# The order of three accumulated slots inside a convolution step

## The chip, the cores and the metric

The kernel runs on one core of a Trainium2 chip. The metric is the device time of one execution in microseconds (us); the median of several executions is compared, and one execution is profiled.

## What is computed

The reference is a chain of four layers on x of shape (4, 32, 32, 16). Each layer first normalises x over groups of two channels and all pixels (`_gn`) and adds its result to x. Layers 0, 1 and 3 have the same core, and nearly all the time is theirs:

```python
first   = jnp.einsum('ijyx,byxc->bijc', Msq, inputs)
shifted = lax.conv_general_dilated(x_nchw, kern, STRIDES, PADDING)   # a 3x3 kernel for each of 32*32*16 outputs
diff    = jax.nn.relu(inputs[:, None, None, :, :, :] - shifted)
second  = L * jnp.einsum('ijyx,bijyxc->bijc', Wsq, diff)
return first - second
```

For each of 1024 output positions (i, j) and 16 channels f there is an own 3x3 kernel over 16 input channels. It is run over the whole 32x32 image, the result is subtracted from the normalised input, cut at zero, weighted with 1024 weights and summed to one number. Layer 2, the interval layer, is a small dynamic program over pairs (i, j), and takes little time of its own.

## The kernel before, in words

The four images are handled as two groups of two (NG, GB). The three convolution layers for two groups make six phases, run one after the other by `conv_layer` (line 436). What the next phase needs (normalisation, the unrolled image, the interval layer) and the `first` term are issued in small pieces between the steps of the running phase: `behind` is a generator, and after each step it is asked for its next piece when a count of steps (`wait`) has run down. The order on every engine is therefore written by hand.

The image is unrolled into `im`: 128 partitions, 64 for each half of the image (16 rows of pixels, 512 pixels). In the 64 partitions of a half stand four taps times 16 input channels. Slot 0 of `im` holds taps 0 to 3, slot 1 taps 4 to 7, and slot 2 the ninth tap alone, four copies of its 16 channels. The kernels' coefficients come in `raw` in the same layout, for a unit of eight output channels and 128 output positions at a time (`load_raw`, line 74, three units ahead, four buffers).

Slots 0 and 1 are multiplied in float32. The profile counts two matmul passes for each such matmul. The ninth tap uses its four copies for another way to float32 accuracy: the tensors `W9` (from `raw`) and `im9` (from `im`) are of type float32r and hold the rounded values in some copies and the remainders in others, so one pass adds up the partial products. They are made by `halve` on ScalarE (line 111) and `halve_rest` on VectorE (line 114). For the weights that is `prep` (line 134, called at the second of a unit's eight channels for the next unit) and `prep_rest` (line 149, called at the fifth); `prep` also lets GpSimd subtract `pick` from slot 1 (line 140), which brings in the input itself. For the image it stands at the end of `before_conv` (lines 232 and 234). At the start of the kernel both pairs are made before step 0: `im9`, then `prep(0)` and `prep_rest(0)` (lines 517 and 518). The loads of slot 2 of `im` are issued first in `before_conv`, then those of taps 0 to 7.

A step is one output channel f and one image b for 128 output positions: six matmuls of 64 x 128 by 512 pixels, three slots for each of two halves (line 463), into a pair of PSUM banks `ps` (three pairs, line 58). The two halves use different halves of TensorE's rows and different banks. Then VectorE takes the pair of banks in one instruction (`scalar_tensor_tensor`, line 473: the smaller of the value and zero, times the 1024 weights of `WT`, summed into a column of `acc`). There are 6 phases x 8 tiles x 16 channels x 2 images = 1536 steps. Between steps TensorE also gets the matmuls of `first_term` (`pf`, line 248, and `pfs`, line 256), and those of the interval layer (`ps_r`, `ps_l`, `ps_y`).

In a step, the first matmul starts the sum in its bank (`start`), and so it is the one that waits until VectorE has read the pair of banks three steps before; the last one (`stop`) tells VectorE to begin. The instructions of a step on TensorE are issued in the order of the loops, and that is the order that the change touches.

Of the kernel before, what the change touches and what calls it, by code (L numbers as in the profile page):

```python
# [37 lines left out]
def net_kernel(ctx: ExitStack, tc: tile.TileContext, x, convs, iv_w, iv_b, out):  # L38
# [19 lines left out]
    def bank_pair(name):  # L58
        return psum.tile([P, 2, 512], F32, tag="ps", name=name)
# [14 lines left out]
    def load_raw(u):  # L74
        if u < n_chunks * NU:
            n = u // NU
            raws[u] = wpool.tile([P, 3, FU, P], F32, tag="raw", bufs=4, name=f"raw_{u}")
            nc.sync.dma_start(raws[u], convs[phases[n // NT][1]][2][n % NT, u % NU])

    def load_chunk(n):  # L80
        if n < n_chunks:
            t = n % NT
            chunks[n] = wpool.tile([P, NP], F32, tag="WT", name=f"WT_{n}")
            nc.sync.dma_start(chunks[n], convs[phases[n // NT][1]][1][t * P : (t + 1) * P, :])
# [49 lines left out]
    def prep(u):  # L134

        if u >= n_chunks * NU:
            return
        raw = raws.pop(u)
        f0 = u % NU * FU
        nc.gpsimd.tensor_tensor(  # L140
            raw[:, 1], raw[:, 1],
            pick[:, f0 : f0 + FU].unsqueeze(2).to_broadcast([P, FU, P]),
            ALU.subtract,
        )
        W9 = wpool.tile([P, FU, P], F32R, tag="W9", name=f"W9_{u}")
        halve(W9, raw[:, 2], low_w)
        units[u] = (raw, W9)

    def prep_rest(u):
        if u in units:  # L150
            raw, W9 = units[u]
            halve_rest(W9, raw[:, 2], low_w)
# [52 lines left out]
    def before_conv(g, layer, on_pe=False):  # L205
        xn = work.tile([P, NT, GC], F32, tag="xn", bufs=2, name=f"xn_{g}_{layer}")
        xns[g] = xn
        yield from group_norm(g, f"c{g}{layer}", xn, on_pe)

        nc.vector.transpose(
            xt[g][:, :, 1 : 1 + H], xn
        )
        inner = xs[g][:, HP : HP + H * HP].rearrange("p (t r n) -> p r t n", r=ROWS, n=HP)
        for r in range(ROWS):
            (nc.scalar if r % 2 else nc.sync).dma_start(inner[:, r], xt[g][GC * r : GC * (r + 1)])
        yield 2
        xsv = xs[g].rearrange("(b c) n -> c b n", b=GB)
        at = 0  # L220
        for slot, row, tap in [(2, row, 8) for row in range(4)] + [
            (tap // 4, tap % 4, tap) for tap in range(8)
        ]:
            for h in range(2):
                off = (HI * h + tap // 3) * HP + tap % 3
                r0 = 64 * h + C * row
                (nc.scalar, nc.sync)[at % 2].dma_start(  # L227
                    im[g][r0 : r0 + C, slot, :, :RUN], xsv[:, :, off : off + RUN]
                )
                at += 1  # L230
        yield 9
        halve(im9[g], im[g][:, 2], low_x)
        yield 2
        halve_rest(im9[g], im[g][:, 2], low_x)
# [201 lines left out]
    def conv_layer(phase, behind):  # L436

        g, layer = phases[phase]
        wait = 0
        imv = im[g].rearrange("p s b (y x) -> p s b y x", x=HP)  # L440
        im9v = im9[g].rearrange("p b (y x) -> p b y x", x=HP)
        acc = work.tile([P, NT, GC], F32, tag="acc", bufs=2, name=f"acc_{phase}")
        for t in range(NT):
            n = phase * NT + t
            for f in range(C):
                u = n * NU + f // FU
                if f % FU == 1:
                    prep(u + 1)
                    load_raw(u + 3)
                if f % FU == 4:  # L450
                    prep_rest(u + 1)
                if f == 2:
                    load_chunk(n + 1)
                W, W9 = units[u]
                for b in range(GB):


                    ps = bank_pair(f"pc_{n}_{f}_{b}")
                    for slot in range(3):
                        for h in range(2):  # L460
                            r = slice(64 * h, 64 * h + 64)
                            w, v = (W9[r], im9v[r, b]) if slot == 2 else (W[r, slot], imv[r, slot, b])
                            nc.tensor.matmul(  # L463
                                ps[:, h, :],
                                lhsT=w[:, f % FU, :],
                                rhs=v[:, :, :H],
                                start=slot == 0,
                                stop=slot == 2,
                            )

                    col = b * C + f
                    junk = work.tile([P, NP], F32, tag="junk", name=f"junk_{n}_{col}")
                    nc.vector.scalar_tensor_tensor(  # L473
                        junk,
                        ps.rearrange("p h n -> p (h n)"),
                        0.0,
                        chunks[n],
                        op0=ALU.min,
                        op1=ALU.mult,
                        accum_out=acc[:, t, col : col + 1],  # L480
                    )
                    wait -= 1
                    if wait <= 0:
                        wait = next(behind, 1 << 20)
            nc.vector.tensor_tensor(X[g][:, t], X[g][:, t], acc[:, t], ALU.add)  # L485
        for _ in behind:
            pass
# [21 lines left out]
    start = before_conv(*phases[0], on_pe=True)  # L509
# [9 lines left out]
    for phase in range(len(phases)):  # L519
        conv_layer(phase, behind(phase))  # L520
# [64 lines left out]
```

## Time and profile before

| | us |
|---|---|
| median of 4 executions | 3105.47 (3105.25 to 3106.09) |
| the profiled execution | 3105.36 |
| its span, first to last instruction | 3103.6 |
| TensorE busy with matmuls (PE) | 3071.3 (99%) |
| TensorE loading weights (PEld) | 1534.2 (49%) |
| VectorE busy (DVE) | 2116.0 (68%) |
| GpSimd (POOL) | 294.7 (9%) |
| ScalarE (ACT) | 145.7 (5%) |

The span is split into engines: PE are matmul passes, PEld the loads of their weights, which run beside them. Two passes of the two halves run side by side, so the sum of the durations of all passes is larger than the busy time. A row of the costliest groups reads: line, engine, operation, output <- inputs, shape, count | busy time, mean duration in ns | idle time of the engine just before such instructions, and what ended most of it. A row of the order of time reads: start and duration in us, engine, line, operation, tensors, count, and in brackets the idle time before it with what ended it. Consecutive instructions of one kind are merged into one row. In the rows `pc<-im,raw` is a float32 pass of slot 0 or 1, and `pc<-im,W` the ninth tap's pass.

### The profile page before, as it was taken

The numbers are of one execution on the slowest core, as the hardware profiler recorded it, in microseconds if no ns is written. First come the engines' busy times: TensorE is split into PE (matmuls) and PEld (weight loads), VectorE is DVE, ScalarE is ACT, GpSimd is POOL, SyncE is SP. The second block draws the span as 40 slices with busy tenths as digits, with TensorE's granted clock in tenths as the row PEclk, the third lists the DMA queues.
The fourth block names the chain that finished last, engine by engine and source line by source line (L and its number), as shares of the span: only waits on it lengthen the run. The fifth ranks groups of instructions, "written<-read, shape, count | busy, mean of one in ns | idle before, by whom it ended". The sixth has DMA issues, their size and how long they took to land.

```text
span 3103.6 us, 37902 instructions
## 1 busy us (share of the span) xinstructions
PE 3071.3 (99%) x15760; PEld 1534.2 (49%) x15760; DVE 2116.0 (68%) x3361; ACT 145.7 (5%) x151; POOL 294.7 (9%) x182
## 2 busy tenths in 40 slices
PE   6999999999999999999999999999999999999999
PEld 4644444444444444444445444444544444444444
DVE  4666666766666666666678876668876666666666
ACT  0000000000000000000000000000000000000000
POOL 1100000100000000000012310001330000000000
PEclk9999999999999999999999999999999999999999
DMA  4331111321111141211111114121113211121100
GB/s 143 125 120 57 48 69 48 125 75 61 55 53 70 48 146 48 75 48 68 48 51 72 48 69 125 48 75 48 68 48 106 95 48 70 48 75 48 68 28 2
DMA packets 37069, 215.19 MB, mean 69 GB/s; under 512 B 11809, under 2 KB 12321, under 8 KB 23073
## 3 DMA queue, kind: packets, MB, share of 16 engines
q1 hardware_dynamic: 29472, 207.02, 18.5%
q10 hardware_dynamic: 7296, 5.74, 0.8%
q8 instruction: 123, 2.02, 0.3%
q14 instruction: 50, 0.40, 0.0%
q0 software_dynamic: 128, 0.02, 0.0%
HBM read 211.64 MB, written 1.12 MB: 69 GB/s over the span
## 4 chain that ended last, share of the span: by engine, by line
PE 99%; DMA 1%; DVE 0%; issue 0%; ACTq 0%; ACT 0%; DVEq 0%
PE pc L463 97%; PE pf L248 1%; PE pfs L256 0%; DMA im<-xs 0%; DMA X<-in_x 0%; DVE junk L473 0%; PE ps_r L376 0%; DMA xs<-xt 0%; PE ps_l L365 0%; PE ps_l L363 0%; DVE xc_c L188 0%; DVE pp L323 0%; ACTq L227 0%; PE ps_y L427 0%; PE ps_vc L178 0%
## 5 line engine op out<-in xcount | busy, mean ns | idle before, releaser
L463 PE MATMUL pc<-im,raw 64*128 64x512 f32 x12288 | 2913.2, 589 | 16.3 <-DMA im<-xs 14.5
L473 DVE SCALAR_TENSOR_TENSOR junk<-pc,WT 128x1024 f32<-128x1024 f32 x1536 | 1880.1, 1224 | 958.7 <-PE pc L463 953.0
L463 PEld LDWEIGHTS pc<-im,raw 64*128 64x128 f32 x12288 | 1209.4, 186 | 1165.7 <-issue 775.0
L463 PE MATMUL pc<-im,W 64*128 64x512 f32 x3072 | 1257.9, 804 | 0.0
L463 PEld LDWEIGHTS pc<-im,W 64*128 64x128 f32 x3072 | 304.8, 186 | 359.6 <-issue 352.2
L140 POOL TENSOR_TENSOR raw<-raw,pick 128x1024 f32<-128x1024 f32 x96 | 182.7, 1905 | 1988.4 <-DMA raw<-in_g 1863.9
L111 ACT ACTIVATE W<-raw,low_w 128x1024 fp32r<-128x1024 f32 x96 | 110.4, 1150 | 2270.6 <-PE pc L463 2234.5
L114 DVE SCALAR_TENSOR_TENSOR W<-raw,low_w,W 128x1024 fp32r<-128x1024 f32 x96 | 136.0, 1416 | 0.0
L473 DVE DVE_READ_ACCUMULATOR junk<-pc,WT 128x1 f32 x1536 | 127.8, 83 | 0.0
L396 POOL TENSOR_TENSOR dp_a<-ft_a,rt_r 128x1089 f32<-128x1089 f32 x16 | 39.1, 2447 | 76.3 <-DVE s_a L403 49.5
L396 POOL TENSOR_TENSOR dp_b<-ft_b,rt_r 128x1089 f32<-128x1089 f32 x16 | 37.1, 2326 | 94.6 <-ACT ft_b L389 47.8
L248 PE MATMUL pf<-MT,xn 128*32 128x512 f32 x192 | 23.1, 598 | 0.0
L403 DVE TENSOR_REDUCE s_b<-dp_b 128x33 f32<-128x1089 f32 x16 | 20.5, 1282 | 0.0
L403 DVE TENSOR_REDUCE s_a<-dp_a 128x33 f32<-128x1089 f32 x16 | 20.5, 1282 | 0.0
L175 POOL PARTITION_ALL_REDUCE sum_mc<-part_mc x5 | 2.2, 447 | 191.5 <-DVE part_mc L167 191.5
L252 ACT COPY fs<-pf 128x512 f32<-128x512 f32 x12 | 7.0, 586 | 240.7 <-PE pf L248 240.7
L114 DVE SCALAR_TENSOR_TENSOR im<-im,low_x,im 128x1088 fp32r<-128x1088 f32 x6 | 8.1, 1348 | 14.0 <-DMA im<-xs 14.0
L485 DVE TENSOR_TENSOR X<-X,acc 128x32 f32<-128x32 f32 x48 | 11.9, 247 | 1.5
L256 PEld LDWEIGHTS pfs<-stack,fs 128*128 128x128 f32 x96 | 11.2, 191 | 3.4 <-issue 3.4
L338 DVE TENSOR_TENSOR pp<-pp 64x1024 f32<-64x1024 f32 x10 | 12.1, 1212 | 0.0
L343 DVE TENSOR_TENSOR pp<-pp 64x1024 f32<-64x1024 f32 x10 | 12.1, 1212 | 0.0
L248 PEld LDWEIGHTS pf<-MT,xn 128*32 128x32 f32 x192 | 5.0, 109 | 14.0 <-issue 14.0
(77 smaller groups left out, 132.9 us busy)
## 6 DMA issues: line engine op xcount, KB each, us to landing
raw<-in_g SPq DMA_DIRECT2D x96, 1536.0 KB, 6.7
WT<-in_w SPq DMA_DIRECT2D x48, 512.0 KB, 6.5
MT<-in_mt SPq DMA_DIRECT2D x12, 2048.0 KB, 8.2
im<-xs SPq DMA_DIRECT2D x72, 67.8 KB, 3.0
im<-xs ACTq DMA_DIRECT2D x72, 67.8 KB, 3.1
xs<-xt SPq DMA_DIRECT2D x12, 34.0 KB, 2.9
xs<-xt ACTq DMA_DIRECT2D x12, 34.0 KB, 3.1
X<-in_x ACTq DMA_DIRECT2D x2, 128.0 KB, 5.1
```

The costliest lines, as they stand in the source:

```text
L111: nc.scalar.activation(dst, src, AF.Copy, scale=mask[:, 1:2])
L114: nc.vector.scalar_tensor_tensor(dst, src, mask[:, 0:1], dst.bitcast(F32), op0=ALU.mult, op1=ALU.add)
L140: nc.gpsimd.tensor_tensor(raw[:, 1], raw[:, 1], pick[:, f0 : f0 + FU].unsqueeze(2).to_broadcast([P, FU, P]), ALU.subtract,)
L248: nc.tensor.matmul(ps[32 * j : 32 * j + 32, :], lhsT=xn[:, pt, :], rhs=mt[:, pt, :], start=pt < 4, stop=pt >= 4, tile_position=(0, 32 * j),)
L256: nc.tensor.matmul(ps[:, GC * t : GC * (t + 1)], lhsT=fs[:, t // 4, t % 4 * P : (t % 4 + 1) * P], rhs=stack, start=True, stop=True,)
L338: nc.vector.tensor_tensor(pp[k][:, :H, M:], a[:, :H, M:], a[:, s : H + s, M:], ALU.max)
L343: nc.vector.tensor_tensor(pp[k][:, :H, M:], a[:, :H, M:], a[:, :H, M - s : M - s + H], ALU.max)
L396: nc.gpsimd.tensor_tensor(t, ft[:, i, :].unsqueeze(1).to_broadcast([P, T1, T1]), rt, ALU.add,)
L403: nc.vector.tensor_reduce(s[:, i - 1, :], last, axis=AX.X, op=ALU.max)
L463: nc.tensor.matmul(ps[:, h, :], lhsT=w[:, f % FU, :], rhs=v[:, :, :H], start=slot == 0, stop=slot == 2,)
L473: nc.vector.scalar_tensor_tensor(junk, ps.rearrange("p h n -> p (h n)"), 0.0, chunks[n], op0=ALU.min, op1=ALU.mult, accum_out=acc[:, t, co ...
L485: nc.vector.tensor_tensor(X[g][:, t], X[g][:, t], acc[:, t], ALU.add)
```

## The change

The loop over the slots runs in the order 2, 0, 1 in place of 0, 1, 2. The ninth tap's matmuls now start the sum in their bank, and those of slot 1 end it. Nothing else is changed; the number of instructions of each kind stays as it is.

```diff
-                    for slot in range(3):
+                    for k, slot in enumerate((2, 0, 1)):
                         for h in range(2):
                             r = slice(64 * h, 64 * h + 64)
                             w, v = (W9[r], im9v[r, b]) if slot == 2 else (W[r, slot], imv[r, slot, b])
@@
                                 ps[:, h, :],
                                 lhsT=w[:, f % FU, :],
                                 rhs=v[:, :, :H],
-                                start=slot == 0,
-                                stop=slot == 2,
+                                start=k == 0,
+                                stop=k == 2,
                             )
```

## The prediction

> **What bounds the kernel now.** I read the page from the top, then the chain that ended last, the costliest groups, and last the order of time in three stretches. The chain and the groups:
>
> ```profile
> PE 99%; DMA 1%; DVE 0%; issue 0%; ACTq 0%; ACT 0%; DVEq 0%
> ...
> L463 PE MATMUL pc<-im,raw 64*128 64x512 f32 x12288 | 2913.2, 589 | 16.3 <-DMA im<-xs 14.5
> L473 DVE SCALAR_TENSOR_TENSOR junk<-pc,WT 128x1024 f32<-128x1024 f32 x1536 | 1880.1, 1224 | 958.7 <-PE pc L463 953.0
> ...
> L463 PE MATMUL pc<-im,W 64*128 64x512 f32 x3072 | 1257.9, 804 | 0.0
> ```
>
> The reader is to see that the end is set by TensorE alone (99% of the chain), that VectorE has 958.7 us to spare, nearly all spent waiting for these matmuls, and that TensorE's only idle time of any size stands at the start (14.5 us, on the loads of im). There are 1536 steps; each has 12288 / 1536 = 8 float32 passes (two per slot and half) and 2 passes of the ninth tap (W). The two halves run side by side, so a step is four float32 passes and one W pass after another.
>
> The order of time in a steady step (start, duration; PEld are weight loads, which start when the pass before begins to stream):
>
> ```profile
> 504.37 0.43 PEld L463 LDWEIGHTS pc<-im,raw 64*128 64x128 f32 x4 [0.24 <-DVE junk L473]
> 504.60 1.88 PE L463 MATMUL pc<-im,raw 64*128 64x512 f32 x8
> 504.81 1.23 DVE L473 SCALAR_TENSOR_TENSOR junk<-pc,WT 128x1024 f32<-128x1024 f32 x1 [0.73 <-PE pc L463]
> 505.04 0.19 PEld L463 LDWEIGHTS pc<-im,raw 64*128 64x128 f32 x2 [0.24 <-issue]
> 505.47 0.19 PEld L463 LDWEIGHTS pc<-im,raw 64*128 64x128 f32 x2 [0.24 <-issue]
> 505.89 0.19 PEld L463 LDWEIGHTS pc<-im,W 64*128 64x128 f32 x2 [0.24 <-issue]
> 505.92 0.80 PE L463 MATMUL pc<-im,W 64*128 64x512 f32 x2
> 505.96 0.08 DVE L473 DVE_READ_ACCUMULATOR junk<-pc,WT 128x1 f32 x1
> 506.32 0.19 PEld L463 LDWEIGHTS pc<-im,raw 64*128 64x128 f32 x2 [0.24 <-DVE junk L473]
> ```
>
> The period is 506.32 - 504.37 = 1.96 us (by the unrounded starts 1.962 over all undisturbed steps), and 1536 of them are 3013 of the 3104 us. The float32 passes follow each other at 0.43 (505.04, 505.47, 505.89, 506.32). W streams from 506.32, when the load behind it starts; the float32 pass behind it starts 0.24 after such a load (504.37 to 504.60, 0.238 unrounded). At the same rate one W pass would be half a float32 pass, 0.213. So 0.025 us per step are lost between W and the float32 pass that follows it.
>
> The start, TensorE's passes:
>
> ```profile
> 26.82 2.28 PE L463 MATMUL pc<-im,raw 64*128 64x512 f32 x4 [14.07 <-DMA im<-xs]
> 29.54 2.27 PE L463 MATMUL pc<-im,raw 64*128 64x512 f32 x4 [0.45 <-DMA im<-xs]
> 30.98 1.26 PE L463 MATMUL pc<-im,W 64*128 64x512 f32 x2
> 31.81 3.12 PE L463 MATMUL pc<-im,raw 64*128 64x512 f32 x7
> ```
>
> and the weight loads of the same stretch:
>
> ```profile
> 30.98 0.29 PEld L463 LDWEIGHTS pc<-im,W 64*128 64x128 f32 x2 [0.74 <-DVE W L114]
> 31.38 0.99 PEld L463 LDWEIGHTS pc<-im,raw 64*128 64x128 f32 x4
> ...
> 34.34 0.30 PEld L463 LDWEIGHTS pc<-im,W 64*128 64x128 f32 x2 [0.26 <-issue]
> 34.77 1.41 PEld L463 LDWEIGHTS pc<-im,raw 64*128 64x128 f32 x8
> ```
>
> Here the four float32 passes of step 0 run from 26.82 on, while ScalarE and VectorE still halve im9 and W9 (line 114's W ends at 30.93). Passes take 0.85 each until 34.3 and 0.43 from then on: the clock is granted at 34.3.
>
> **The change part by part.** No instruction is added or removed. The built programs have the same order on VectorE, ScalarE, GpSimd and SP; on TensorE every step now has its two W matmuls ahead of its float32 ones, and TensorE's separate semaphore instructions fall from 108 to 18, since the waits for a new unit no longer fall on one instruction. The first steps of units are no longer than others in the trace (1.962 both), so these 90 are worth nothing.
>
> *Steady steps: 0.* The order in time is a ring: raw raw raw raw W raw raw raw raw W. The change cuts the ring in another place, but W still follows a float32 pass and is followed by one, so the 0.025 us stay. What moves is the new bank, the start flag and the wait for VectorE: from the float32 pass behind W to W, behind a float32 pass. No row of before has this pairing. What speaks for nothing: at 34.77 the load behind W carries no wait, and its pass starts at 35.01, also 0.24 later; so the wait is not what costs. While the clock was half, the pass behind W started 31.81 - 31.38 = 0.43 after its load, which is the W pass alone at half clock (2 x 0.213): with the same new bank, nothing was lost. A loss by the bank or the flag should show there too; a load of 0.19 plus 0.05 that is too long for 0.213 but not for 0.43 fits both rows. And where a float32 pass follows a float32 pass of another bank, in the interval layer:
>
> ```profile
> 1671.47 0.46 PE L376 MATMUL ps_r<-r,r 64*128 64x363 f32 x1
> 1671.70 0.66 PE L463 MATMUL pc<-im,raw 64*128 64x512 f32 x2
> ```
>
> the ps_r pass has 363 columns, 0.43 x 363 / 512 = 0.30, and ends at 1671.77; the later of the two pc passes starts at 1671.70 + 0.66 - 0.59 = 1671.77, on time, in a new bank. So I take 0. The ends: if the pairing behaves like the worst seen, all of the excess is paid again (0.025, and 0.005 in the pass behind it, 0.433 against 0.428), 0.03 x 1536 = +46 us; if the excess belongs to the new bank behind a short pass, it goes, -46 us.
>
> The Trainium skill, "TensorE: Matmul & The Clock Gate", section "LDWEIGHTS (loading the stationary operand)", gives 128 columns / 1.2 = 107 ns for a load, against 186 ns in the groups of this trace. By 107 the load would hide behind 213, the excess would have another cause, and the change could win it: 3062 us. The trace's load is the longer one, and it decides.
>
> *Waits and covers: 0.* W's first load now waits for the PSUM buffer, with all later loads and matmuls queued behind it. VectorE frees a step's buffer at 505.96 + 0.08 = 506.04; the step that takes it (three buffers) loads at 506.32 + 1.96 = 508.28, so 2.24 are spare. The new first load is issued at the start of a float32 pass instead of a W pass, 0.43 - 0.24 = 0.19 earlier. The smallest spare time in the trace, but for one step where TensorE does stall (1.8 us at 1617.5, on VectorE), is 0.33 us, so no new stall. Without that cover each step would show its missing part, at most 0.19. W9 of the next unit is finished from the fifth of a unit's eight channels on (prep_rest, line 451), 4 x 2 steps or some 15 us before its use, which now is one step's float32 passes earlier. The loads of raw get one W pass more.
>
> *Breaks: +0.4.* Where another layer's matmuls (12 groups pf, 6 pfs, about ten in the interval layer) end a step, W now always pays 0.24 instead of 0.213 at the end, at most 0.03 each, 0.8 in all; half of it, as the drain behind a float32 pass is a little shorter than that behind W.
>
> *The start: +2.4.* W comes first and waits for line 114 at 30.93 as before. It streams from about 31.15 (an empty array needs about 0.15 for the load) and the float32 passes follow at 31.6 instead of 31.81, but all four of step 0 are still to be done. Until 34.34 the new order does (34.34 - 31.6) / 0.85 = 3.2 of them; the old one had done 4 + 3.0. It is 3.8 passes behind, at full clock 3.8 x 0.43 = 1.6 us. That is if the clock comes at the same moment. Before, it came 4.8 us after the unbroken work began (29.54) and 7.5 after the first conv matmul. Counted from 30.98 that is 35.8 or 38.5, 1.45 or 4.2 late, and each late us costs half: +0.7 or +2.1. Ends 1.6 and 3.7; I take 4.8 us of unbroken work, 2.4.
>
> By the skill's same page, "Part 1: The HAM clock gate", a free-running window of 3.4 us must be busy; from 30.98 that opens the gate between 34.4 and 37.8, a cost of 1.6 to 3.3. No run here shows the window itself.
>
> *The end: 0.* Behind the last pass VectorE starts after the same drain.
>
> Sum: the profiled execution took 3105.36 (span 3103.6, 1.8 around it): 3105.36 + 0 + 0.4 + 2.4 = 3108.2. It stands 0.1 below the median of the runs, 3105.47, which I leave aside.
>
> **Rivals.**
> Faster (0.08): the 0.03 us behind W belong to starting a new bank behind a short pass. For it: in the steady rows both always come together. Against it: the half-clock row. 3108.2 - 46 = 3062.
> Slower (0.10): a first load that carries the wait and a new group is not taken ahead behind a float32 pass as smoothly as the plain W load is. Price as above, 0.03 a step, +46: 3154; it decides from 4 ns a step on (6.2 us). For it: no row of before shows this pairing. Against it: the load at 504.37 carries the same wait and costs what the one at 34.77 does.
> That the change does not do what it says can be left out: the built order shows W first in every step.
>
> **How the numbers follow.** No change within 0.2% (6.2 us, about what a measurement of this kernel can tell): 0.82; faster 0.08; slower 0.10, in which a clock granted very late has a small part. The likeliest case spans the start's ends and a little for the one stall: 3104.5 to 3112. It holds about 8 in 10, so the range stops there; the two ends of the pairing at 3062 and 3154 lie in what is left out.
>
> **What would show it.** Right: a period of 1.96 with W loaded 0.43 ahead of the step and a load 0.24 ahead of the float32 pass behind it; the first conv matmul at 31.0; the clock at full near 36. Wrong: a period of 1.93 or 1.99 in the steady steps, or new idle time of TensorE on VectorE in the interval layers.

## The result, and the profile after

The changed kernel takes 3108.31 us (median of 41 executions, 3105.42 to 3109.97) against 3105.42 (61 executions, 3101.66 to 3108.32): ratio 1.0009, 95% interval 1.0005 to 1.0014, that is 1.6 to 4.3 us more. The forecast was 3108.2 and no change within 0.2%. The number is right; the sum behind it is right only in part.

The page after, chain by engine and the costliest groups on TensorE:

```profile
PE 99%; DMA 1%; DVE 0%; issue 0%; SPq 0%; ACTq 0%; ACT 0%; DVEq 0%
...
L463 PE MATMUL pc<-im,raw 64*128 64x512 f32 x12288 | 2904.8, 589 | 0.0
...
L463 PE MATMUL pc<-im,W 64*128 64x512 f32 x3072 | 1246.0, 799 | 20.3 <-DVE W L114 18.5
```

TensorE still sets the end. Its first wait has changed its owner: 18.5 us for line 114, in place of 14.5 us for the loads of im. The order of time at the start, after:

```profile
29.64 1.28 DVE L114 SCALAR_TENSOR_TENSOR W<-raw,low_w,W 128x1024 fp32r<-128x1024 f32 x1
...
30.97 0.79 PE L463 MATMUL pc<-im,W 64*128 64x512 f32 x2 [18.52 <-DVE W L114]
...
31.57 3.60 PE L463 MATMUL pc<-im,raw 64*128 64x512 f32 x8
...
34.12 0.33 PEld L463 LDWEIGHTS pc<-im,W 64*128 64x128 f32 x2 [0.52 <-issue]
...
34.98 0.46 PEld L463 LDWEIGHTS pc<-im,raw 64*128 64x128 f32 x4 [0.52 <-issue]
...
35.25 1.88 PE L463 MATMUL pc<-im,raw 64*128 64x512 f32 x8
```

Line 114 ends when it ended before (29.64 + 1.28 = 30.92, against 30.93). The four float32 passes of step 0 now run from 31.57 to 34.98, 0.85 each, all at half clock; the trace puts the grant of the clock at 35.02, against 34.30.

A steady step, after:

```profile
504.84 0.44 PEld L463 LDWEIGHTS pc<-im,raw 64*128 64x128 f32 x4 [0.24 <-issue]
...
505.52 0.19 PEld L463 LDWEIGHTS pc<-im,raw 64*128 64x128 f32 x2 [0.24 <-issue]
505.95 0.19 PEld L463 LDWEIGHTS pc<-im,raw 64*128 64x128 f32 x2 [0.24 <-issue]
...
506.38 0.19 PEld L463 LDWEIGHTS pc<-im,W 64*128 64x128 f32 x2 [0.24 <-DVE junk L473]
...
506.81 0.19 PEld L463 LDWEIGHTS pc<-im,raw 64*128 64x128 f32 x2 [0.24 <-issue]
```

The wait for VectorE (`<-DVE junk L473`) has moved from the float32 load to W's load, 0.43 ahead of the float32 load behind it, as forecast. To the eye the period is the old one, 1.97 here. But one row of the chain that ended last covers the same 199 steps without a break in both kernels (start, duration). Before:

```profile
243.67 390.56 PE pc L463 x1990
```

and after:

```profile
245.65 390.89 PE pc L463 x1990
```

The changed kernel is 1.98 us late where this stretch begins and loses another 0.33 in it, 1.66 ns a step. Over all undisturbed steps the mean periods are 1961.7 and 1963.2 ns. So the difference of the two profiled spans, 3107.9 - 3103.6 = 4.3 us, is made up so: at step 2 the new order is 2.20 behind by the load of the first float32 pass (36.97 against 34.77), of which 0.24 is the W pass that it has done and the old order has not, so the start costs 1.96; from step 2 to the end another 2.31 are added, and 1.5 ns x 1534 steps is 2.3. Nothing is left for the breaks, the places where another layer's matmuls stand between two steps.

Executions of one kernel spread over 4 to 7 us. One source can be seen in the traces: in either of the two interval layers (near 1617 and 2137 us) VectorE's line 114 can fall beside GpSimd's work and take 4.27 us instead of 1.28, and TensorE then waits 1.77 us:

```profile
1612.01 4.27 DVE L114 SCALAR_TENSOR_TENSOR W<-raw,low_w,W 128x1024 fp32r<-128x1024 f32 x1
...
1617.48 1.99 PE L463 MATMUL pc<-im,raw 64*128 64x512 f32 x8 [1.77 <-DVE junk L473]
```

These rows are of the kernel before. It happens once in each of the two profiles compared, and none to two times in those of the experiments. Spans of single profiles are therefore not compared below; starts, undisturbed stretches and medians are.

### The profile page after: what moved, and what is told of

It is laid out like the page before. It is cut to its first block, busy times and chain, and to the rows that moved or that the text cites. A ratio compares the mean times of both kernels' runs of the same rounds, so it can differ in the third digit from the quotient of the medians.

```text
span 3107.9 us, 37812 instructions
## 1 busy us (share of the span) xinstructions
PE 3071.9 (99%) x15760; PEld 1511.8 (49%) x15760; DVE 2118.1 (68%) x3361; ACT 145.6 (5%) x151; POOL 294.9 (9%) x182
## 3 DMA queue, kind: packets, MB, share of 16 engines
q1 hardware_dynamic: 29472, 207.02, 18.5%
## 4 chain that ended last, share of the span: by engine, by line
PE 99%; DMA 1%; DVE 0%; issue 0%; SPq 0%; ACTq 0%; ACT 0%; DVEq 0%
PE pc L463 97%; PE pf L248 1%; PE pfs L256 0%; DMA im<-xs 0%; DMA X<-in_x 0%; PE ps_r L376 0%; DVE junk L473 0%; PE ps_l L365 0%; DMA xs<-xt 0%; PE ps_l L363 0%; DVE xc_c L188 0%; DVE im L114 0%; DVE pp L323 0%; DVE W L114 0%; SPq L227 0%
## 5 line engine op out<-in xcount | busy, mean ns | idle before, releaser
L473 DVE SCALAR_TENSOR_TENSOR junk<-pc,WT 128x1024 f32<-128x1024 f32 x1536 | 1879.9, 1224 | 960.9 <-PE pc L463 954.9
L463 PEld LDWEIGHTS pc<-im,raw 64*128 64x128 f32 x12288 | 1194.8, 186 | 1156.6 <-issue 1078.6
L463 PE MATMUL pc<-im,W 64*128 64x512 f32 x3072 | 1246.0, 799 | 20.3 <-DVE W L114 18.5
L473 DVE DVE_READ_ACCUMULATOR junk<-pc,WT 128x1 f32 x1536 | 127.8, 83 | 0.0
```

The source lines that it names most:

```text
L463: nc.tensor.matmul(ps[:, h, :], lhsT=w[:, f % FU, :], rhs=v[:, :, :H], start=k == 0, stop=k == 2,)
L473: nc.vector.scalar_tensor_tensor(junk, ps.rearrange("p h n -> p (h n)"), 0.0, chunks[n], op0=ALU.min, op1=ALU.mult, accum_out=acc[:, t, co ...
```

## The experiments

**Which part is it?** The theory after the result: start (theory A) and steps (theory B) each bring about half. The rival: it is the start alone, and the 1.5 ns are chance. First, the changed kernel with step 0 in the old order:

```diff
-                    for k, slot in enumerate((2, 0, 1)):
+                    for k, slot in enumerate((0, 1, 2) if n + f + b == 0 else (2, 0, 1)):
```

> The changed kernel with step 0 of all 1536 back in the order 0, 1, 2. Theory A (most of the +2.9 us is the start: four float32 passes of step 0 that no longer run while W9 and im9 are made): the time returns to before, +0 to +0.7 us, first conv matmul at 26.8 again, and step 2 begins as early as in the kernel before but for one W pass. Theory B (the steady steps: the profile after has a mean period 1.5 ns longer, 1963.2 against 1961.7, 2.3 us over the kernel, and this belongs to the new order): +2 us or more remain.

Measured: 3106.96 against 3104.93, ratio 1.0007 (0.9999 to 1.0016). The start is that of before: first conv matmul at 26.50, line 114 done 0.32 earlier than in the kernel before, and step 2 0.30 earlier once the W pass is taken off. The stretch of 199 steps takes exactly what it takes in the changed kernel:

```profile
243.52 390.89 PE pc L463 x1990
```

So theory A alone falls: 1.5 ns a step belong to the new order, and come back to the hundredth of a us in another execution. Then the kernel before with step 0 alone in the new order:

```diff
-                    for slot in range(3):
+                    for k, slot in enumerate((2, 0, 1) if n + f + b == 0 else (0, 1, 2)):
```

> The kernel before with step 0 alone in the order 2, 0, 1. Theory A: nearly the whole change, +2.0 to +2.6 us, first conv matmul at 31.0 and the clock granted near 35. Theory B: less than half of it, since all other steps are in the old order.

Measured: 3106.68 against 3104.93, ratio 1.0005 (0.9996 to 1.0013). The weight loads at its start:

```profile
30.32 0.29 PEld L463 LDWEIGHTS pc<-im,W 64*128 64x128 f32 x2 [17.64 <-DVE W L114]
...
33.48 0.34 PEld L463 LDWEIGHTS pc<-im,raw 64*128 64x128 f32 x2 [0.52 <-issue]
34.07 0.19 PEld L463 LDWEIGHTS pc<-im,raw 64*128 64x128 f32 x2 [0.26 <-issue]
```

The clock came at 33.8, only 3.5 us after the first conv matmul; counted from the end of line 114 (30.27), the start costs 1.7 us, a little less than theory A alone would have and more than theory B. Its stretch of 199 steps:

```profile
244.56 390.56 PE pc L463 x1990
```

is that of the old order to the hundredth. The two differences to before, 2.0 and 1.75, add up to 3.8, which lies in the interval of the whole change; each alone is at the edge of what the medians can tell, and the answer rests on the stretches of 199 steps.

**What is lost behind W?** The prediction blamed the load behind it. Theory L says so; theory S blames the step from a float32r pass to a float32 one. This run has image 0's steps in the old order and image 1's in the new, so that two W passes meet:

```diff
-                    for slot in range(3):
+                    for k, slot in enumerate((2, 0, 1) if b else (0, 1, 2)):
```

> The steps of image 0 in the order 0, 1, 2, those of image 1 in the order 2, 0, 1, so that two ninth-tap passes stand together and then eight float32 passes. Theory L (a ninth-tap pass lasts 0.238 in place of 0.213 because the weight load behind it is longer than the pass): both W passes still take 0.238, the period stays at 1.962, the time is that of before, within 0.05%. Theory S (the step from a float32r pass to a float32 pass costs 25 ns, whatever the load): one such step in two is gone, 12 ns a step, -19 us, 0.6% faster. Start as in the kernel before, no loss there.

Measured: 3101.25 against 3104.93, ratio 0.9990 (0.9981 to 0.9999), no -19 us. The loads where two W passes meet:

```profile
839.51 0.19 PEld L463 LDWEIGHTS pc<-im,W 64*128 64x128 f32 x2 [0.24 <-issue]
...
839.94 0.19 PEld L463 LDWEIGHTS pc<-im,W 64*128 64x128 f32 x2 [0.24 <-DVE junk L473]
840.18 0.43 PEld L463 LDWEIGHTS pc<-im,raw 64*128 64x128 f32 x4
```

The first W pass streams from 839.94 to 840.18, 0.24, though another W pass follows: theory S falls. That the mean period is 1960.0, shorter than in either order, and the time 3.7 us less, theory L did not say.

Next, W between the two float32 slots:

```diff
-                    for slot in range(3):
+                    for k, slot in enumerate((0, 2, 1)):
```

> Order 0, 2, 1 in every step: W stands between two float32 passes of its own bank, and the new bank begins behind a float32 pass of the slot 1. Theories L and S: same period, 1.962. A cost of new banks or of the wait would show as a period other than in both kernels. Theory A for the start: the two passes of slot 0 run early, the two of slot 1 come behind W, so +0.8 to +1.3 us. In all +0 to +1.5 us.

Measured: 3108.78 against 3104.93, ratio 1.0014 (1.0005 to 1.0023), more than was expected. The period is 1962.2, and the start 1.1 us late. That is about 2 of the 3.9 us; the slow line 114 comes up in both interval layers of this profile, which may be the rest, but is not shown for the other executions. Each order has a period of its own, within 3.2 ns of the others. New banks and waits are no common cause, since here they stand behind float32 passes as in the changed kernel, at another period.

**Where do 240 and 248 come from?** In the trace of the changed kernel the W pass lasts 248 ns in image 0's steps and 240 in image 1's, throughout (from the start of the load behind it to the start of the next load). Theory D says that where W reads its pixels decides which, theory P that the place of the step does. First, both images' W passes read image 0's pixels:

```diff
-                            w, v = (W9[r], im9v[r, b]) if slot == 2 else (W[r, slot], imv[r, slot, b])
+                            w, v = (W9[r], im9v[r, 0]) if slot == 2 else (W[r, slot], imv[r, slot, b])
```

> The changed kernel, in which the ninth-tap pass of image 1 reads image 0's im9 (so the ninth tap of image 1 is left out and image 0's counted twice). In the profile after, the W pass of image 0's steps lasts 0.248, that of image 1's 0.240, throughout; this alternation is the whole of the longer mean period (1963.2 against 1961.7 ns). Theory D (where the pass reads its pixels decides): the alternation goes and all steps have one period, 1958 or 1968. Theory P (the place of the step, or something else of it, decides): alternation and mean of 1963.2 stay.

Measured: 3106.75 in one execution. W lasts 238 in image 0's steps, 244 in image 1's, mean period 1960.1. Neither theory had that: what the pass reads matters, as the numbers moved, but an alternation stays. Then the images in the other order:

```diff
-                for b in range(GB):
+                for b in (1, 0):
```

> The changed kernel with image 1's step ahead of image 0's. Theory D: the long W pass (0.248) stays with image 0, which is now the second step of each pair. Theory P: it stays with the first step of each pair. Mean period 1963.2 in both.

Measured: 3111.49 in one execution, period 1963.2. The 248 stay with image 0, now the second step of the pair. That fits theory D and speaks against P. Then a shorter load behind W:

```diff
                             nc.tensor.matmul(
-                                ps[:, h, :],
-                                lhsT=w[:, f % FU, :],
+                                ps[: P - 32 * (k == 1), h, :],
+                                lhsT=w[:, f % FU, : P - 32 * (k == 1)],
```

> The changed kernel in which slot 0 has 96 weight columns in place of 128 (slot 0 is left out for a quarter of the output positions), so the loads behind the W pass are shorter, by a quarter or about 45 ns; no pass streams less. Theory L (the W pass lasts 0.24 because the load behind it takes 0.19 and 0.05 more): the load ends before the 0.213 of the pass, W lasts 0.216, the period falls to about 1.937, -38 us. If the excess is not the load's: period unchanged at 1.963.

Measured: 3111.26 in one execution, period 1963.3. The loads behind W, where they stand alone, are

```profile
842.35 0.16 PEld L463 LDWEIGHTS pc<-im,raw 64*96 64x96 f32 x2 [0.24 <-issue]
```

160 ns in place of 186: less of a cut than the 45 ns expected, but by theory L enough (0.160 + 0.05 = 0.21). The W pass still takes 240 and 248. The stretch of 199 steps shows it best:

```profile
245.16 390.89 PE pc L463 x1990
```

the same as with the whole load. Theory L, and with it the prediction's reading, falls here. Theory D is not shown either: in this run the 248 stand in image 1's steps and the 240 in image 0's, though W reads the same pixels in the same order as in the changed kernel. What decides which image has the longer pass stays open. Last, the two float32 slots exchanged:

```diff
-                    for k, slot in enumerate((2, 0, 1)):
+                    for k, slot in enumerate((2, 1, 0)):
```

> The changed kernel with the two float32 slots exchanged, order 2, 1, 0: the load behind W now reads the weights of slot 1, and its pass the pixels of slot 1. If the addresses of the pass behind W decide the 0.248 and 0.240: another pattern and another mean period, between 1958 and 1968. If not: the same alternation by image and 1963.2.

Measured: 3109.37 in one execution, period 1963.2 with the same alternation by image. Which slot the float32 pass behind W loads and reads does not matter. What was left to try is how W's own pixels lie.

**How W's pixels lie.** In the kernels so far a row of 32 pixels in `im9` is 34 elements, 136 bytes, from the next. The new theory R: the W pass, which reads 512 pixels in some 240 ns, can't be fed as fast as it could go from such rows; the float32 passes, which take 429 ns for as many, can. `im9` without the two spare columns needs no more work than before:

```diff
-    im9 = [const.tile([P, GB, PITCH], F32R, name=f"im9{g}") for g in range(NG)]
+    im9 = [const.tile([P, GB, HI, H], F32R, name=f"im9{g}") for g in range(NG)]
...
-        halve(im9[g], im[g][:, 2], low_x)
+        src = im[g][:, 2].rearrange("p b (y x) -> p b y x", x=HP)[:, :, :, :H]
+        halve(im9[g][:, :, :, :H], src, low_x)
...
-        halve_rest(im9[g], im[g][:, 2], low_x)
+        halve_rest(im9[g][:, :, :, :H], src, low_x)
...
-        im9v = im9[g].rearrange("p b (y x) -> p b y x", x=HP)
+        im9v = im9[g]
```

In the built programs `im9` of the first group, to which most of the stretch of 199 steps belongs, begins at the same address, a multiple of 64, whatever its rows; only the tensors behind it move with its size. In the order of the changed kernel:

> The changed kernel with im9 stored without the gaps between the image's rows (16 rows of 32 pixels side by side, in place of rows 34 apart), so that the W pass reads 512 pixels in one run; results as before. Theory R (the W pass lasts 0.240 to 0.248 in place of 0.213 because of how its pixels are read at one per cycle: 16 short rows, or their addresses): W lasts about 0.216, the period falls to about 1.935, 28 ns x 1536 = -43 us against the changed kernel. Theory F (27 ns belong to a float32r pass as such, or to a least time between a load and its pass that does not depend on the load's length): 0.240 or more stays, and the time with it.

Measured: 3086.54 against 3105.98, ratio 0.9941 (0.9928 to 0.9953). And in the order of before:

> The kernel before with the same im9 without gaps. Theory R: period 1.935, -41 us against before, 3064. Theory F: 3105. Against the kernel above in both theories: faster by the start, 1.7 to 2.0 us, and under R without the 1.5 ns a step between the two orders, since both come from the reading of W's pixels.

Measured: 3088.01 against 3105.98, ratio 0.9943 (0.9930 to 0.9957). Both beat both kernels; which of the two is faster, these medians do not tell. The 1.7 to 2.0 us by which the old order was to start ahead are not seen in them: with five executions each, the new order is 1.5 us faster, within their spread. The stretch of 199 steps (the line number has moved by one) in the new order

```profile
244.83 388.25 PE pc L464 x1990
```

and in the old

```profile
241.20 388.25 PE pc L464 x1990
```

The W pass falls to 230 to 238 ns, the float32 pass behind it from 433 to 429, and the periods are 1950.0 in both. Theory R is right in direction and takes half of its size: -11.7 and -13.2 ns a step where some -27 were expected. And the 1.5 ns between the two orders are gone, though waits, banks and flags still differ between them: the 1.5 ns do not come from these by themselves, but need the rows as they lay. Two runs ask what is left. A shorter load again, on top of the new order with the gaps closed (slot 0 with 96 columns as above):

> The changed order with im9 without gaps and, as in the run with the short load, 96 weight columns in slot 0 (slot 0 is left out for a quarter of the output positions). With im9 without gaps W still lasts 0.230 to 0.238, 17 to 25 ns more than half a float32 pass. Theory L (what is left is the load behind W, 0.186 and some 0.043): a load 26 ns shorter brings W near 0.216, period 1.934, another -25 us. Theory F (what is left belongs to the float32r pass or to a least time between load and pass): W stays at 0.230 to 0.238, period 1.950.

Measured: 3082.95 in one execution, period 1946.7:

```profile
244.61 387.59 PE pc L464 x1990
```

0.66 us less in 199 steps, 3.3 ns a step instead of 16: W lasts about 230 or 234 and no longer 237. A small part is the load's, most is not. And rows 48 elements, 192 bytes, apart, in the old order:

```diff
-    im9 = [const.tile([P, GB, HI, H], F32R, name=f"im9{g}") for g in range(NG)]
+    im9 = [const.tile([P, GB, HI, 48], F32R, name=f"im9{g}") for g in range(NG)]
```

> The old order with the rows of im9 48 pixels (192 bytes) apart in place of 34 (136 bytes). If the jump from row to row is what the W pass pays for, it stays near 0.240 to 0.246 and the period near 1.962; if it is where the rows begin (136 bytes apart, most rows lie across one more boundary of 64 bytes), it falls to that of im9 without gaps, 1.950.

Measured: 3090.42 in one execution:

```profile
242.99 388.25 PE pc L464 x1990
```

As fast as without gaps, though it jumps after every row. So the jump costs nothing; where the rows begin does. 128 and 192 are both multiples of 64, while 136 is a multiple of 8 only: which boundary between the two counts was not tried. That slow feeding is what lengthens the pass is the theory's picture; the traces show the times, not the reads.

## Why the prediction was right, and where it was wrong

**What bounds the kernel:** right; TensorE stays the chain's 99%.

**Steady steps: 0:** this is the step that failed. It said that W still follows a float32 pass and is followed by one, "so the 0.025 us stay". They changed by 1.5 ns, 2.3 us in all, more than half of the 4.3 us between the two profiles. The bounds held (0.03 a step either way), and the rivals at the ends did not come: no cost near 30 ns went or came, so a new bank or the wait behind a short pass is not what costs. But the cause that was named, "a load of 0.19 plus 0.05 that is too long for 0.213 but not for 0.43", was argued from two rows that another cause fits as well. A load 26 ns shorter changed nothing with the old rows of im9, and 3.3 ns with the new. A pass that is fed too slowly at full clock could well be fed in time at half clock, too: that row never told the two apart. With rows that begin at multiples of 64 bytes the period falls by 12 to 13 ns whatever the order; so much of the excess belongs to how W's pixels lie, and only the 3.3 ns can be laid on the load.

The Trainium skill, "TensorE: Matmul & The Clock Gate", section "LDWEIGHTS (loading the stationary operand)", was weighed there and set aside, since its 107 ns stood against 186 in the trace. The run with 96 columns shows 160: 26 ns for 32 columns, 0.81 a column, and the page's 1 / 1.2 is 0.83. The record of a load contains some 80 ns besides (186 - 107). Since a shorter load changed nothing, the page's number seems the better measure of what has to be hidden. By it the excess had "another cause", which is what the runs found; that the change could win it back was not so.

**Waits and covers: 0:** right. In the interval layers the smallest spare time before a first load, but for the one stall, falls from 0.33 to 0.13 us, much as the 0.19 of the working say. Only two steps show W's load waiting for VectorE in a new place (near 85.8 and 117.1 us, 0.15 and 0.11, behind a line 114 that took 3.0 us), and the steps behind them are shorter by as much: about 1 ns is left.

**Breaks: +0.4:** too high. Between step 2 and the end the steps explain all of the 2.31 us.

**The start: +2.4:** the right mechanism; the size was 1.96, and 1.7 where step 0 was changed alone. Its working gives 1.6 plus half of the clock's delay; the delay was 0.72 and not 1.45, and 1.6 + 0.36 is 1.96. Where step 0 was changed alone the clock came only some 0.15 later, counted from the end of line 114, and 1.6 + 0.07 is 1.7. Taken wrong was that the clock comes 4.8 us after unbroken work begins. Over all runs it came between 32.3 and 35.4 us with the first conv matmul near 26.5, and between 33.8 and 36.4 with it near 31: 6.0 to 8.8 us after it in the first case, where TensorE idles once more for 0.3 to 1.9 us before line 114 is done, and 3.3 to 5.6 in the second, where it does not. A fixed delay does not fit this. The skill's free-running window (same page, "Part 1: The HAM clock gate") could spread the delays so; its 3.4 us from a window's start to its end are not seen by themselves here.

**The sum:** 2.8 was forecast, the medians say 2.9, the two profiles 4.3. That the number came out right owes something to chance: start and breaks were 0.8 too high, the steps 2.3 too low, and the rest lies in the spread of executions, of which TensorE's 1.77 us behind the slow line 114 are a part.

What stays open: why the orders differ by up to 3.2 ns while rows of im9 lie 136 bytes apart, which of the two images has the longer W pass in the changed order, and the 16 to 24 ns that the W pass takes above half a float32 pass (214 ns) even with rows that begin well.

## What to carry to other kernels

When passes follow each other without a gap, changing which of them opens the sum moves little but what stands at the ends: look for the first one's operands, and for what else could run while they are made. A few ns of excess per pass are worth a look at how the moving operand lies: here dense rows gave 18 to 19 us, six times what the order did. Two rows that fit an explanation do not confirm it while they fit another; a run that shortens the suspect alone can tell them apart.

## What the runs showed of the hardware

The float32r pass of 512 pixels takes 238 to 248 ns with rows of 32 pixels 136 bytes apart, 230 to 238 with rows 128 or 192 bytes apart. A float32 pass takes 429 ns, and 433 behind a W pass that reads rows 136 bytes apart; the float32 passes' own rows were 136 bytes apart in every run. Periods of steady steps repeat between executions to less than 0.1 ns (199 steps in 390.56 twice, in 390.89 four times and once more with another load), so that a single profile tells 1 ns a step, where medians of times that spread over 4 to 7 us can't.
